# A transformer block on one core: the MLP's first tiles are normed and turned in projection 1, and MLP weights are issued by another queue

## The chip, the cores and the metric

The kernel runs on one core of a Trainium2 chip. Its engines are TensorE (PE, matmuls; PEld is its weight load), VectorE (DVE), ScalarE (ACT), GpSimd (POOL) and SyncE (SP, which only issues transfers). ACT and POOL also issue transfers, each on a queue of its own. The metric is device time in microseconds (us), as the median of several runs. A smaller number is better.

## The reference

One block of a diffusion transformer: x has 2 batches of 2048 tokens with 576 features, in fp32. A condition vector gives six rows (shift, scale and gate for attention and for the MLP).

```
mod = silu(c) @ w_ada + b_ada
sh_msa, sc_msa, g_msa, sh_mlp, sc_mlp, g_mlp = split(mod, 6)
xn = ln(x, 1e-6) * (1 + sc_msa) + sh_msa
q, k, v = (xn @ w_qkv + b_qkv)          # 16 heads of 36
q, k = ln(q) * qn_g + qn_b, ln(k) * kn_g + kn_b
o = softmax(q @ k^T * scale) @ v
x = x + g_msa * (o @ w_proj + b_proj)
xn2 = ln(x, 1e-6) * (1 + sc_mlp) + sh_mlp
x = x + g_mlp * (gelu(xn2 @ w1 + b1) @ w2 + b2)   # 576 -> 2304 -> 576
```

## The kernel before

Tokens are taken in tiles of 128 (16 tiles for each batch, `NT`) and in blocks of four tiles (`TPB` = 4, 512 tokens). The stages run one after the other: inputs of batch 0 (norm, modulation, QKV), attention 0, projection 1 (`outputs(0, ...)`), inputs of batch 1, attention 1, projection 2 (`outputs(1, ...)`), the MLP's first product over all 8 blocks of both batches, and its second product.

**Turning a tile.** A matmul wants the features on the partitions. A tile of rows is therefore measured (`bn_stats` twice, `bn_aggr`, a square root on ACT, a reciprocal), normed in one operation, transposed in squares of 32 x 32 by DVE, and stored to DRAM by four transfers that put the squares in place (`squares_turned`, L894 and L899; the DRAM tile is `turned`). `turned_loaded` (L907, L909) then loads it, transposed, into the tile `xnt` and its tail part by three transfers, and `turned_modulated` applies scale and shift with ACT, and POOL adds the shift of the tail part (L393).

**A projection** (`outputs`) takes token tiles in groups of four, one PSUM tile (`s_tile`, two banks) for each of four; so tile t + 4 can start only when tile t's PSUM has been read. That is done by DVE: `evicted` multiplies the PSUM tile with the gate row into `product` (L1260). `summed` adds `product` to the rows of x1 (x plus bias, gated, which attention prepared in DRAM; L1267), stores x1 (POOL, L1268), and `residual` loads the rows of a later tile (POOL, L1255). The matmuls of a group stand in the order: `whole` of the first two tiles, `halved` of all four (the last 64 features), `whole` of the last two. `placed(t)` runs whatever work another stage has asked to have in between.

**The order of the work.** Inside a `manual_schedule` the named engines run in the order of the code. Elsewhere a scheduler puts each engine's instructions in order. DVE's order is written out in `inputs`, in projection 2 and in the MLP, and during attention also that of POOL and ACT; projection 1 has the scheduler's order on all engines. [...]

**Around the change.** In attention, each pair of heads p, block of queries and group of keys is a step, and `hooks` hang other work on a step. During the last pair of attention 1, `rows_opened` loads the first five tiles of batch 0's x1 back from DRAM, further hooks measure one each, and `rows_turned` at the step (7, NBLK - 1, NG - 1) norms and turns them, with the stores on ACT, SP and POOL in turn. In attention 0 the same hooks do this with the first two tiles of batch 1's x. The rows stand in `spare`, twelve slices of a tile that attention doesn't need by then. Projection 2 keeps x1 in nine `scratch` tiles; between its tiles, DVE forms sums of the MLP's weights: `wb` comes in four quarters of 1152 KB (issued at L1447 on SP, with the loads of the five turned tiles between them) for sums at L1464 to L1467, and `last_rows`, the last 64 rows (576 KB, L1455), is cast and summed at L403 and L404.

**The MLP's first product** has 72 jobs (8 blocks times 9 parts of the hidden features). It uses seven products of sums for four block products, so that DVE forms token sums for every block (`token_sums`, L1511 to L1514), and evicts each job with four operations (L1568 to L1575) ahead of a gelu on ACT and a store by SP. `ahead(job)` loads, turns, reads back and modulates the tiles of the next block, at job numbers given by offsets.

Of the kernel before, what the change touches and what calls it, by code (L numbers as in the profile page):

```python
# [16 lines left out]
P = 128  # L17
# [14 lines left out]
def dit_block(  # L32
# [233 lines left out]

    x_first = const.tile([P, C + 64], F32, name="x_first")

    def rows_normed(pool, xt, repeated=True):
        st = pool.tile([P, 2, 6], F32, name="st", bufs=2)  # L270
        for a in range(2):
            nc.vector.bn_stats(st[:, a, :], xt[:, a * HALF : (a + 1) * HALF])
        mv = pool.tile([P, 2], F32, name="mv", bufs=2)
        nc.vector.bn_aggr(mv, st.rearrange("p a s -> p (a s)"))
        std = pool.tile([P, 1], F32, name="std", bufs=2)
        nc.scalar.activation(std, mv[:, 1:2], AF.Sqrt, bias=eps6)
        rstd = pool.tile([P, 1], F32, name="rstd", bufs=2)
        nc.vector.reciprocal(rstd, std)
        nc.vector.tensor_scalar(xt[:, :C], xt[:, :C], mv[:, 0:1], rstd, ALU.subtract, ALU.mult)  # L279
        if repeated:  # L280
            nc.scalar.copy(xt[:, C:], xt[:, 512:576])
        return xt[:, :512], xt[:, 512:]
# [472 lines left out]
    def block_of_small():  # L755
# [487 lines left out]
                nc.gpsimd.tensor_tensor(rows, rows, spare[2], ALU.add)  # L1243
                nc.gpsimd.dma_start(out=x1_dram[b, (t - 1) * P : t * P, :], in_=rows)

        def outputs(b, weights, between, scratch):


            wp, wp4, g1, pool = weights
            x1s = {}  # L1250

            def residual(t):
                if t < NT:
# [9 lines left out]
            def summed():  # L1263
                while products:
                    t, product = products.pop(0)
                    x1 = x1s.pop(t)
                    nc.vector.tensor_tensor(x1, x1, product, ALU.add)  # L1267
                    nc.gpsimd.dma_start(out=x1_dram[b, t * P : (t + 1) * P, :], in_=x1)  # L1268
                    residual(t + 6)

            def placed(t):
                for do in between.get(t, ()):
# [5 lines left out]
            for t0 in range(0, NT, 4):  # L1278
                tiles, sums = [], []
                for t in range(t0, t0 + 4):  # L1280
                    if t < t0 + 2:
                        placed(t)
                    ps = s_tile()
                    tiles.append(ps)
                    sums.append((
                        [ps[:, a, :HALF] for a in range(2)],
                        lambda k, a, t=t: qo[:, k, t * P : (t + 1) * P],
                        lambda k, a: wp[:, k, a * HALF : (a + 1) * HALF] if k < FULL else wp4[:, 0, :],
                    ))
                    if t < t0 + 2:  # L1290
                        whole(*sums[-1], True)
                summed()
                for i, sum_ in enumerate(sums):
                    halved(*sum_, i >= 2)
                evicted((t0, t0 + 1))
                placed(t0 + 2)
                summed()
                whole(*sums[2], False)
                evicted((t0 + 2,))
                placed(t0 + 3)  # L1300
                whole(*sums[3], False)
                evicted((t0 + 3,))
# [9 lines left out]
        for b in range(B):  # L1312
# [44 lines left out]
            }  # L1357
            if b + 1 < B:
                begun = [(spare[9 + t], x[b + 1, t * P : (t + 1) * P, :], spare[7 + t]) for t in range(2)]
            else:  # L1360
                begun = [
                    (spare[3 + j], x1_dram[0, j * P : (j + 1) * P, :], spare[(8 + j) % len(spare)])
                    for j in range(TPB + 1)
                ]

            def rows_opened():
                opening["begun"] = rows_begun(begun)
                for i in range(len(begun)):
                    opening["begun"][0](i)

            def rows_turned():
                opening["turned"] = opening["begun"][2]()

            hooks |= {(7, 1, 1): rows_opened, (7, NBLK - 1, NG - 1): rows_turned}
            hooks |= {
                (7, 2 + i // NG, i % NG): lambda i=i: opening["begun"][1](i) for i in range(len(begun))
            }
            if b == 0:
                hooks |= {
                    (0, 2, 1): ada_opened,  # L1380
# [12 lines left out]
            if b + 1 < B:  # L1393
                weights, close_weights = input_weights()
                first_turned, rows = opening["turned"]
                xnt = input_loaded(first_turned, nc.sync)
                outputs(b, wp, {12: [lambda: input_modulated(b + 1, xnt)]}, spare)
                close_wp()


# [39 lines left out]
        slot = {1: 0, 2: 2, 3: 3, 4: 6, 5: 4, 6: 5, 7: 1}  # L1440

        wr = [mw.tile([P, MH], F32R, name=f"wr{i}") for i in range(3)]
        rows4, close_rows4 = opened("rows4")
        last_rows = rows4.tile([64, 2, MH], F32, name="last_rows")
        first = opening["turned"]
        for i, (k, f) in enumerate(((0, 0), (0, 1), (1, 0), (1, 1))):
            nc.sync.dma_start(  # L1447
                out=wb[:, i],
                in_=w1[k * PAIR : (k + 1) * PAIR, f * MH : (f + 1) * MH].rearrange("(k p) f -> p k f", p=P),
            )  # L1450
            for j in (2 * i, 2 * i + 1):
                if j <= TPB:
                    n, t = divmod(j, TPB)
                    turned_loaded(xnts[n], slice(t * P, (t + 1) * P), first[j], nc.sync)
        nc.sync.dma_start(out=last_rows, in_=w1[512:576, :].rearrange("p (a f) -> p a f", a=2))  # L1455
        left, right = last_rows[:, 0], last_rows[:, 1]
        last_parts = [
            lambda: weight_parts(wr[0], left),
# [24 lines left out]
            between.setdefault(t + 1, []).append(last_parts[i])  # L1483
        in_order = tc.manual_schedule(engines={mybir.EngineType.DVE})
        in_order.__enter__()
        scratch, close_scratch = opened("scratch")
        outputs(B - 1, wp, between, [scratch.tile([P, C], F32, name=f"x1_{i}") for i in range(9)])
        close_scratch()
        close_rows4()
        close_wp()  # L1490
        close_outs()
        close_xs()
# [89 lines left out]
        def ahead(job):  # L1582
# [3 lines left out]

            def at(**offsets):
                for i in range(TPB):
                    read = max(0, 2 * i - 1)
                    for what, offset in offsets.items():  # L1590
                        m, g = divmod(job - read - offset, HF)
                        if g == 0 and m + 1 < NB and (m, i) > (0, 0):
                            yield what, (m + 1, i)

            for what, todo in at(turn=-2, read=0, modulate=2, load=-5):
                m, i = todo
                block, cols = xnts[m % 2], slice(i * P, (i + 1) * P)
                if what == "load":
# [5 lines left out]
                else:  # L1604
                    turned_modulated(block, cols, 2, m // NBLK)

        for m, k, n in ((2, 0, 0), (5, 1, 1), (3, 0, 1), (4, 1, 0)):
            quarter = w2[k * HF * P : (k + 1) * HF * P, n * HALF : (n + 1) * HALF]
            nc.sync.dma_start(out=ws[m], in_=quarter.rearrange("(f p) c -> p f c", p=P))
        later_sums = [  # L1610
            lambda: nc.vector.tensor_tensor(ws[6], ws[2], ws[3], ALU.add),
            lambda: nc.vector.tensor_tensor(ws[3], ws[3], ws[5], ALU.subtract),
# [8 lines left out]
        rows_ahead = {}  # L1621
        for i in (1, 2):
            rows_ahead[1, i] = mlp_loaded(1, i, nc.gpsimd)
        rows_ahead[1, 1] = tile_turned(rows_ahead[1, 1], nc.gpsimd)
        token_sums(0)
        for job in range(0, NB * HF, 2):
            (n0, f0), (n1, f1) = divmod(job, HF), divmod(job + 1, HF)
# [11 lines left out]
            gelu_stored(n1, f1, 1)  # L1639
            if job % 4 == 2 and job > 2 * HF and later_sums:  # L1640
                later_sums.pop(0)()
            if job == 4 * HF:
                hidden_loaded(0)
        stack.close()
# [139 lines left out]
```

## Time and profile before

| what | us |
|---|---|
| median of 3 runs (lowest to highest) | 3205.18 (3202.65 to 3205.25) |
| the profiled execution | 3209.03 |
| its span in the profile | 3207.2 |
| PE busy | 3159.1 |
| inputs 0, attention 0 | 0 to 254, to 1033.6 |
| projection 1, inputs 1 | to 1105.1, to 1330.8 |
| attention 1, projection 2 | to 2104.5, to 2198.1 |
| MLP's first product, second product | to 2711.6, to 3200.5 |

The stages' bounds are read from PE's timeline. A row of the waits view reads "engine, operation's output, line, what it waited for: us in total, times, longest". A timeline row has the start, the duration, engine and line, operation, tiles and shapes, how many (x), and in brackets the idle time before it with what ended it. A `q` behind an engine's name (SPq) is its issuing of transfers.

### The profile page before, as it was taken

To read this page: it belongs to the slowest core of one execution; us is meant where nothing else is said; L and a number is where in the kernel's file an instruction comes from. 1 tells how busy PE (TensorE), PEld (TensorE's weight loads), DVE (VectorE), ACT (ScalarE), POOL (GpSimd) and SP (SyncE) were. 2 spreads that over 40 slices of the span, in tenths; PEclk is the share of its full clock that TensorE was granted. 3 is DMA by queue.
4 is the path that set the end of the run, shared out by engine and by line. 5 is a ranking of instruction groups with operands and counts; after the bars stand their busy time and mean duration, and the time that the engine had idled before them with its cause. 6 is when DMAs were issued, how large, how long until landed. Compare 5 with 4: busy or idle time off the path is not lost. (4 is left out here: it accounts for less than half of the span.)

```text
span 3207.2 us, 47334 instructions
## 1 busy us (share of the span) xinstructions
PE 3159.1 (98%) x17833; PEld 1895.6 (59%) x17833; DVE 1510.2 (47%) x2213; ACT 1505.3 (47%) x2941; POOL 657.2 (20%) x922
## 2 busy tenths in 40 slices
PE   7999999999999999999999999989999999999999
PEld 5884333333334788633333333357888888777777
DVE  5774333333333478533333333436566554455454
ACT  2336666666666034466666666632555542000000
POOL 4551000111110255300001111023334320122111
PEclk9999999999999999999999999999999999999999
DMA  4222212233222522121222222265555433333331
GB/s 149 76 65 68 75 35 69 62 74 83 65 76 51 169 69 70 39 65 31 50 57 64 66 68 65 64 195 183 151 143 131 132 110 129 133 133 111 118 104 38
DMA packets 163641, 291.51 MB, mean 91 GB/s; under 512 B 43715, under 2 KB 95884, under 8 KB 161292
## 3 DMA queue, kind: packets, MB, share of 16 engines
q1 hardware_dynamic: 112116, 176.37, 18.1%
q0 software_dynamic: 44176, 111.15, 13.4%
q8 instruction: 143, 2.34, 0.3%
q10 hardware_dynamic: 7112, 0.89, 0.2%
q14 instruction: 94, 0.77, 0.1%
HBM read 155.42 MB, written 84.63 MB: 75 GB/s over the span
## 5 line engine op out<-in xcount | busy, mean ns | idle before, releaser
L1127 ACT ACTIVATE pt<-b 128x512 f32<-128x512 f32 x2048 | 1057.6, 610 | 487.0 <-PE b L1136 272.8
L1136 PE MATMUL b<-pt,vt 128*64 128x512 f32 x4096 | 935.0, 598 | 0.0
L1136 PEld LDWEIGHTS b<-pt,vt 128*64 128x64 f32 x4096 | 271.8, 136 | 582.1 <-issue 438.8
L1123 PE MATMUL b<-qm,km 32*128 32x512 f32 x4096 | 568.4, 614 | 0.8 <-DVE vt L1040 0.6
L1184 DVE TENSOR_TENSOR ot<-b,ot 128x512 f32<-128x512 f32 x192 | 132.7, 691 | 643.3 <-PE b L1136 642.9
L1123 PE MATMUL b<-qe,ke 16*128 16x512 f32 x2048 | 423.8, 789 | 0.0
L1029 PE MATMUL s<-wq,xnt 128*128 128x288 f32 x1536 | 405.2, 407 | 6.3 <-DMA wq<-in_w_qkv_dram 5.5
L1123 PEld LDWEIGHTS b<-qm,km 32*128 32x128 f32 x4096 | 191.9, 184 | 270.7 <-ACT pt L1127 208.0
L1696 PE MATMUL s<-ws,as 128*128 128x288 f32 x1440 | 351.8, 406 | 0.0
L1029 PEld LDWEIGHTS s<-wq,xnt 128*128 128x128 f32 x1536 | 281.0, 190 | 68.3 <-DVE xt L279 4.1
L1696 PEld LDWEIGHTS s<-ws,as 128*128 128x128 f32 x1440 | 273.6, 190 | 75.6
L1155 DVE RECIPROCAL den<-den 128x512 f32<-128x512 f32 x64 | 213.5, 3336 | 13.9 <-DMA den<-den_dram 13.9
L1541 PE MATMUL m<-xnt,wb 128*128 128x256 f32 x864 | 211.4, 381 | 4.4 <-DVE cs L1575 3.5
L1541 PE MATMUL m<-s,wb 128*128 128x256 f32 x864 | 211.0, 380 | 2.0 <-DVE s L1511 2.0
L1182 DVE COPY ot<-b 128x512 f32<-128x512 f32 x64 | 44.3, 692 | 331.7 <-PE b L1136 331.7
L899 POOL DMA_DIRECT2D turned<-squares x220 | 147.6, 677 | 222.8 <-DVE squares L894 197.0
L1541 PEld LDWEIGHTS m<-s,wb 128*128 128x128 f32 x864 | 164.7, 191 | 24.9 <-DVE s L1511 2.4
L1123 PEld LDWEIGHTS b<-qe,ke 16*128 16x128 f32 x2048 | 108.3, 184 | 114.5 <-issue 112.7
L1541 PEld LDWEIGHTS m<-xnt,wb 128*128 128x128 f32 x864 | 159.4, 191 | 24.8 <-DVE cs L1575 4.3
L1240 POOL DMA_DIRECT2D kr<-in_x_dram x32 | 17.5, 545 | 720.8 <-DVE met L786 720.8
L1579 ACT ACTIVATE cs<-cs,b_sb 128x512 f32<-128x512 f32 x144 | 99.5, 719 | 113.7 <-DVE cs L1574 90.4
L1696 PE MATMUL s<-ws,hidden 128*128 128x288 f32 x576 | 142.3, 406 | 0.0
(198 smaller groups left out, 2995.6 us busy)
## 6 DMA issues: line engine op xcount, KB each, us to landing
gelu<-cs SPq DMA_DIRECT2D x144, 256.0 KB
hidden<-gelu SPq DMA_DIRECT2D x16, 2304.0 KB
den<-den_dram SPq DMA_DIRECT2D x128, 128.0 KB
turned<-squares POOLq DMA_DIRECT2D x220, 72.0 KB, 2.4
xnt<-turned POOLq DMA_DIRECT2D x56, 256.0 KB, 3.7
x_dram<-kr POOLq DMA_DIRECT2D x48, 288.0 KB, 2.8
qm<-qo SPq DMA_DIRECT2D x192, 64.0 KB
kr<-in_x_dram POOLq DMA_DIRECT2D x34, 288.0 KB, 3.8
```

Source lines behind the costliest of these rows:

```text
L899: queue.dma_start(out=by_square[g], in_=squares[g * SQ : (g + 1) * SQ, :].rearrange("p (k j) -> p k j", j=SQ))
L1029: nc.tensor.matmul(out_a, full[:, k, :], wq[:, k, f], start=k == 0, stop=False)
L1123: nc.tensor.matmul(ps, k[r, keys], q[r, :], start=first, stop=not first)
L1127: nc.scalar.activation(pt[:, h, :], banks[2 * c + h], AF.Exp, scale=SCALE)
L1136: nc.tensor.matmul(acc[64 * h : 64 * h + 64, :], vt[:, v0 : v0 + 64], pt[:, h, :], start=pt is pts[0][0], stop=pt is pts[-1][0],)
L1155: nc.vector.reciprocal(den, den)
L1182: nc.vector.tensor_copy(ot, acc)
L1184: nc.vector.tensor_tensor(ot, acc, ot, ALU.add)
L1240: nc.gpsimd.dma_start(out=spare[t % 2], in_=x[b, t * P : (t + 1) * P, :])
L1541: nc.tensor.matmul(out_m[m], wb[:, slot[m], k, f * P : (f + 1) * P], moving[m](k), start=k == 0 and m in (1, 2, 5, 6), stop=k == 1 and m == 1,
L1579: nc.scalar.activation(part, part, AF.Gelu, bias=b1_sb[:, g : g + 1])
L1696: nc.tensor.matmul(ms[m], stationary[m][:, f, :], ws[m][:, f, :], start=(f == 0), stop=(f == HF - 1))
```

## The change

- `rows_measured` is split from `rows_normed`. `outputs` takes a function `turned_of`; in projection 1 it gives, for tiles 0 to 4, a turning: the tile's x1 is measured after its store is issued, and behind the next `evicted` the new function `turned` norms x1 in place and turns it, with the four stores on POOL. The squares use `spare[9]` to `spare[11]`, and projection 1's x1 rows the first nine of `spare`. DVE's order in projection 1 is now the written one.
- Attention 1 no longer loads, measures and turns these five tiles. In attention 0, the turning of batch 1's two tiles is hung on the step behind the last.
- The MLP's weights `wb` and `last_rows` are issued by ACT; the five loads of turned tiles stay on SP, behind one another.
- The x1 rows of projection 2 are opened ahead of `last_rows`, so they lie where the exponentials (`pt`) of attention were, and `last_rows` lies in memory that is free sooner.
- In the MLP, tile i of the next block is read at job 2i (before max(0, 2i - 1)), modulated one job after (before two). The turn of tile (1, 1) ahead of the first token sums falls out (it comes in job 0). The loads of the four quarters of w2 are written between jobs 2 and 14 and no longer ahead of job 0.

```diff
--- before.py
+++ after.py
@@ -266,7 +266,7 @@
 
     x_first = const.tile([P, C + 64], F32, name="x_first")
 
-    def rows_normed(pool, xt, repeated=True):
+    def rows_measured(pool, xt):
         st = pool.tile([P, 2, 6], F32, name="st", bufs=2)
         for a in range(2):
             nc.vector.bn_stats(st[:, a, :], xt[:, a * HALF : (a + 1) * HALF])
@@ -276,7 +276,11 @@
         nc.scalar.activation(std, mv[:, 1:2], AF.Sqrt, bias=eps6)
         rstd = pool.tile([P, 1], F32, name="rstd", bufs=2)
         nc.vector.reciprocal(rstd, std)
-        nc.vector.tensor_scalar(xt[:, :C], xt[:, :C], mv[:, 0:1], rstd, ALU.subtract, ALU.mult)
+        return mv[:, 0:1], rstd
+
+    def rows_normed(pool, xt, repeated=True):
+        mean, rstd = rows_measured(pool, xt)
+        nc.vector.tensor_scalar(xt[:, :C], xt[:, :C], mean, rstd, ALU.subtract, ALU.mult)
         if repeated:
             nc.scalar.copy(xt[:, C:], xt[:, 512:576])
         return xt[:, :512], xt[:, 512:]
@@ -1243,11 +1247,11 @@
                 nc.gpsimd.tensor_tensor(rows, rows, spare[2], ALU.add)
                 nc.gpsimd.dma_start(out=x1_dram[b, (t - 1) * P : t * P, :], in_=rows)
 
-        def outputs(b, weights, between, scratch):
+        def outputs(b, weights, between, scratch, turned_of=lambda t: None):
 
 
             wp, wp4, g1, pool = weights
-            x1s = {}
+            x1s, to_turn = {}, []
 
             def residual(t):
                 if t < NT:
@@ -1267,6 +1271,14 @@
                     nc.vector.tensor_tensor(x1, x1, product, ALU.add)
                     nc.gpsimd.dma_start(out=x1_dram[b, t * P : (t + 1) * P, :], in_=x1)
                     residual(t + 6)
+                    if turn := turned_of(t):
+                        to_turn.append((turn, x1, rows_measured(xs["pool"], x1)))
+
+            def turned():
+                while to_turn:
+                    turn, x1, scales = to_turn.pop(0)
+                    nc.vector.tensor_scalar(x1, x1, *scales, ALU.subtract, ALU.mult)
+                    turn(x1)
 
             def placed(t):
                 for do in between.get(t, ()):
@@ -1293,10 +1305,12 @@
                 for i, sum_ in enumerate(sums):
                     halved(*sum_, i >= 2)
                 evicted((t0, t0 + 1))
+                turned()
                 placed(t0 + 2)
                 summed()
                 whole(*sums[2], False)
                 evicted((t0 + 2,))
+                turned()
                 placed(t0 + 3)
                 whole(*sums[3], False)
                 evicted((t0 + 3,))
@@ -1357,24 +1371,19 @@
             }
             if b + 1 < B:
                 begun = [(spare[9 + t], x[b + 1, t * P : (t + 1) * P, :], spare[7 + t]) for t in range(2)]
-            else:
-                begun = [
-                    (spare[3 + j], x1_dram[0, j * P : (j + 1) * P, :], spare[(8 + j) % len(spare)])
-                    for j in range(TPB + 1)
-                ]
-
-            def rows_opened():
-                opening["begun"] = rows_begun(begun)
-                for i in range(len(begun)):
-                    opening["begun"][0](i)
-
-            def rows_turned():
-                opening["turned"] = opening["begun"][2]()
-
-            hooks |= {(7, 1, 1): rows_opened, (7, NBLK - 1, NG - 1): rows_turned}
-            hooks |= {
-                (7, 2 + i // NG, i % NG): lambda i=i: opening["begun"][1](i) for i in range(len(begun))
-            }
+
+                def rows_opened():
+                    opening["begun"] = rows_begun(begun)
+                    for i in range(len(begun)):
+                        opening["begun"][0](i)
+
+                def rows_turned():
+                    opening["turned"] = opening["begun"][2]()
+
+                hooks |= {(7, 1, 1): rows_opened, (None, None, None): rows_turned}
+                hooks |= {
+                    (7, 2 + i // NG, i % NG): lambda i=i: opening["begun"][1](i) for i in range(len(begun))
+                }
             if b == 0:
                 hooks |= {
                     (0, 2, 1): ada_opened,
@@ -1394,7 +1403,14 @@
                 weights, close_weights = input_weights()
                 first_turned, rows = opening["turned"]
                 xnt = input_loaded(first_turned, nc.sync)
-                outputs(b, wp, {12: [lambda: input_modulated(b + 1, xnt)]}, spare)
+                first = []
+
+                def turned_of(t):
+                    squares = spare[9 + t % 3]
+                    return (lambda x1: first.append(squares_turned(x1, nc.gpsimd, squares))) if t <= TPB else None
+
+                with tc.manual_schedule(engines={mybir.EngineType.DVE}):
+                    outputs(b, wp, {12: [lambda: input_modulated(b + 1, xnt)]}, spare[:9], turned_of)
                 close_wp()
 
 
@@ -1440,19 +1456,19 @@
         slot = {1: 0, 2: 2, 3: 3, 4: 6, 5: 4, 6: 5, 7: 1}
 
         wr = [mw.tile([P, MH], F32R, name=f"wr{i}") for i in range(3)]
+        scratch, close_scratch = opened("scratch")
+        x1_rows = [scratch.tile([P, C], F32, name=f"x1_{i}") for i in range(9)]
         rows4, close_rows4 = opened("rows4")
         last_rows = rows4.tile([64, 2, MH], F32, name="last_rows")
-        first = opening["turned"]
         for i, (k, f) in enumerate(((0, 0), (0, 1), (1, 0), (1, 1))):
-            nc.sync.dma_start(
+            nc.scalar.dma_start(
                 out=wb[:, i],
                 in_=w1[k * PAIR : (k + 1) * PAIR, f * MH : (f + 1) * MH].rearrange("(k p) f -> p k f", p=P),
             )
-            for j in (2 * i, 2 * i + 1):
-                if j <= TPB:
-                    n, t = divmod(j, TPB)
-                    turned_loaded(xnts[n], slice(t * P, (t + 1) * P), first[j], nc.sync)
-        nc.sync.dma_start(out=last_rows, in_=w1[512:576, :].rearrange("p (a f) -> p a f", a=2))
+        nc.scalar.dma_start(out=last_rows, in_=w1[512:576, :].rearrange("p (a f) -> p a f", a=2))
+        for j in range(TPB + 1):
+            n, t = divmod(j, TPB)
+            turned_loaded(xnts[n], slice(t * P, (t + 1) * P), first[j], nc.sync)
         left, right = last_rows[:, 0], last_rows[:, 1]
         last_parts = [
             lambda: weight_parts(wr[0], left),
@@ -1483,10 +1499,9 @@
             between.setdefault(t + 1, []).append(last_parts[i])
         in_order = tc.manual_schedule(engines={mybir.EngineType.DVE})
         in_order.__enter__()
-        scratch, close_scratch = opened("scratch")
-        outputs(B - 1, wp, between, [scratch.tile([P, C], F32, name=f"x1_{i}") for i in range(9)])
+        outputs(B - 1, wp, between, x1_rows)
+        close_rows4()
         close_scratch()
-        close_rows4()
         close_wp()
         close_outs()
         close_xs()
@@ -1586,13 +1601,12 @@
 
             def at(**offsets):
                 for i in range(TPB):
-                    read = max(0, 2 * i - 1)
                     for what, offset in offsets.items():
-                        m, g = divmod(job - read - offset, HF)
+                        m, g = divmod(job - 2 * i - offset, HF)
                         if g == 0 and m + 1 < NB and (m, i) > (0, 0):
                             yield what, (m + 1, i)
 
-            for what, todo in at(turn=-2, read=0, modulate=2, load=-5):
+            for what, todo in at(turn=-2, read=0, modulate=1, load=-5):
                 m, i = todo
                 block, cols = xnts[m % 2], slice(i * P, (i + 1) * P)
                 if what == "load":
@@ -1604,9 +1618,13 @@
                 else:
                     turned_modulated(block, cols, 2, m // NBLK)
 
-        for m, k, n in ((2, 0, 0), (5, 1, 1), (3, 0, 1), (4, 1, 0)):
+        quarters = [(2, 0, 0), (5, 1, 1), (3, 0, 1), (4, 1, 0)]
+
+        def quarter_loaded():
+            m, k, n = quarters.pop(0)
             quarter = w2[k * HF * P : (k + 1) * HF * P, n * HALF : (n + 1) * HALF]
             nc.sync.dma_start(out=ws[m], in_=quarter.rearrange("(f p) c -> p f c", p=P))
+
         later_sums = [
             lambda: nc.vector.tensor_tensor(ws[6], ws[2], ws[3], ALU.add),
             lambda: nc.vector.tensor_tensor(ws[3], ws[3], ws[5], ALU.subtract),
@@ -1621,7 +1639,6 @@
         rows_ahead = {}
         for i in (1, 2):
             rows_ahead[1, i] = mlp_loaded(1, i, nc.gpsimd)
-        rows_ahead[1, 1] = tile_turned(rows_ahead[1, 1], nc.gpsimd)
         token_sums(0)
         for job in range(0, NB * HF, 2):
             (n0, f0), (n1, f1) = divmod(job, HF), divmod(job + 1, HF)
@@ -1639,6 +1656,8 @@
             gelu_stored(n1, f1, 1)
             if job % 4 == 2 and job > 2 * HF and later_sums:
                 later_sums.pop(0)()
+            if job % 4 == 2 and quarters:
+                quarter_loaded()
             if job == 4 * HF:
                 hidden_loaded(0)
         stack.close()
```

## The prediction

> **What bounds the kernel now.** I read the page's busy shares first, then what TensorE (PE) waits for, then the stages by windows, then every engine's timeline around the waits found.
>
> ```profile
> PE 3159.1 (98%) x17833; PEld 1895.6 (59%) x17833; DVE 1510.2 (47%) x2213; ACT 1505.3 (47%) x2941; POOL 657.2 (20%) x922
> ```
>
> PE is busy in 3159.1 of 3207.2 us. The change removes no matmul, so all it can win is PE's idle time and the time PE runs at a lower clock. The waits view says where the idle time is:
>
> ```profile
> PE s L420 <- DVE product L1260: 17.1, 2, 8.9
> ...
> PE m L1541 <- DVE cs L1575: 3.5, 4, 1.5
> PE m L1541 <- DVE s L1511: 2.0, 1, 2.0
> ```
>
> 17.1 us in two waits stand in projection 2, the rest at the start of the MLP and between its blocks. The windows view has, per stretch, the length, busy time of PE, PEld, DVE, ACT, POOL, then the PE clock, DMA share and GB/s. Projection 1 (1033.6 to 1105.1) and projection 2 (2104.5 to 2198.1) run the same 322 matmuls:
>
> ```profile
> 1033.60:1105.10 71.50, 71.50 (x322) 54.26 (x321) 31.72 (x42) 4.84 (x12) 15.19 (x28) 1.00 0.60 189
> 2104.50:2198.10 93.60, 76.50 (x322) 56.28 (x320) 47.99 (x52) 12.06 (x30) 23.35 (x41) 0.89 0.63 198
> 2133.50:2143.70 10.20, 3.23 (x10) 2.00 (x11) 3.88 (x6) 2.52 (x6) 6.20 (x13) 0.50 0.87 303
> ...
> 2205.20:2208.50 3.30, 3.30 (x9) 2.63 (x8) 2.10 (x6) 1.58 (x2) 1.46 (x3) 0.50 1.04 348
> ```
>
> Projection 2 is 93.60 - 71.50 = 22.1 us longer: 17.1 of waits, and 76.50 - 71.50 = 5.0 of PE time, because after each wait the clock is 0.50 for 10.2 us. Who is late, by VectorE's (DVE) timeline (start, duration, what it waited for):
>
> ```profile
> 2110.23 0.65 DVE L1184 TENSOR_TENSOR ot<-b,ot 128x512 f32<-128x512 f32 x1
> ...
> 2124.72 3.35 DVE L1155 RECIPROCAL den<-den 128x512 f32<-128x512 f32 x1 [10.08 <-DMA den<-den_dram]
> ...
> 2137.74 0.76 DVE L1267 TENSOR_TENSOR x<-x,product 128x576 f32<-128x576 f32 x1 [8.93 <-DMA x<-x_dram]
> ...
> 2165.62 0.75 DVE L403 CAST wr<-last_rows 64x1152 fp32r<-64x1152 f32 x1 [9.88 <-DMA last_rows<-in_w_dram]
> ...
> 2167.93 0.76 DVE L1260 TENSOR_TENSOR product<-s,gate 128x576 f32<-128x576 f32 x1
> ```
>
> DVE runs in written order here. The products that free PE's PSUM tiles stood behind an add that waited 8.93 us for x1 rows, and later behind a cast that waited 9.88 us for MLP weights. So transfers bound it. SyncE's (SP) and GpSimd's (POOL) queues say why they were late:
>
> ```profile
> 2106.25 9.34 SPq L899 DMA_DIRECT2D turned<-kr  x8
> ...
> 2135.16 2.41 SPq L1447 DMA_DIRECT2D wb<-in_w_dram  x4
> 2137.66 1.23 SPq L1455 DMA_DIRECT2D last_rows<-in_w_dram  x1
> ```
> ```profile
> 2133.28 0.45 POOL L393 TENSOR_TENSOR parts<-tail,parts 128x128 fp32r<-128x128 f32 x1 [1.89 <-ACT tail L392]
> 2133.76 1.61 POOL L1255 DMA_DIRECT2D x<-x_dram  x3
> ```
>
> SP spends 9.34 us on the stores of the five turned tiles, then loads these back until 2135, and only then issues the weights. POOL issues the x1 loads behind the modulation's adds, which wait for those loads.
>
> **The Trainium skill.** "TensorE: Matmul & The Clock Gate", Part 1, says that the clock falls to half after an idle window of some 3.4 us and recovers after a busy one. The trace agrees in kind (0.50 after each wait) but not in length: 10.2 us after the long waits, 3.3 after the short pair at the MLP's start (0.90 and 1.96). "DMA: Bandwidth & Descriptors", "Issuing engines are not separate DMA queues": SP and ScalarE (ACT) feed the same 16 engines, so moving an issue saves queueing, not bandwidth; the trace has 0.87 of the engines busy at 303 GB/s in the first slow window. "ScalarE: Activation LUTs", "What ACT_TABLE_LOAD costs": 1283 ns; the trace has 1.28 us.
>
> **What is removed, part by part.** (1) The end of attention 1 loses five loads, five measurings, five norms and transposes of DVE (2103.3 to 2110.2, five times 0.58 + 0.78), and twenty stores. DVE's last ot add then runs at about 2105, not 2110.23. SP is free at about 2104 and issues the xnt loads at once, not between 2120 and 2134. ACT then modulates five tiles from about 2107; at the old pace (five adds of POOL some 2.5 to 3 us apart) that ends at about 2121. POOL's x1 loads follow at 2120.5 rather than 2133.76. The first add came 2137.74 - 2133.76 = 4.0 after; so adds from 2124.5 and product 2 at about 2127. PE first waited at 2140.47 - 8.95 = 2131.5: a margin of 4, gap gone.
>
> (2) The weights wb (four of 1152 KB) follow ACT's modulation, at about 2122 instead of 2135.2. The first sum of two of them ran at 2151.17, 16 after; now about 2138. Four DVE operations behind it (2.56, 1.42, the casts 0.75 and 1.49) put product 7 at about 2146. PE needed it at 2168.74 - 8.12 = 2160.6, which is 2149 to 2150 once the first gap and its slow clock (8.95 + 2.5) are gone: margin about 4. last_rows is no longer awaited (see 4). Projection 2 becomes 71.5: -22.1.
>
> (3) The MLP: the turn of tile (1,1) ahead of the first token sums is gone, a turn being about 3.7 us of DVE by its rows. The 1.96 wait goes, and the 2.0 us that the slow clock added (the first job took 11.0 where others take 7.0: 4.0 less 1.96). Turns of later tiles stand two jobs apart, so no eviction stands behind two of them. In the double turn before 2329, DVE also waited 2.89 for a store (same buffer). The three waits on cs were 0.97, 0.86 and 1.50: -3.3. One turn in 14 us of DVE time has slack, since the gaps came only where two stood together. Total gain: 22.1 + 4.0 + 3.3 = 29.4.
>
> **What is added.** (4) last_rows has memory free early, and the schedule puts its load at the start of attention 1 on ACT, ahead of the exponentials' table load. It waits there for DVE's last v eviction:
>
> ```profile
> 1331.49 1.28 ACT L1127 ACT_TABLE_LOAD   x1
> 1332.79 3.53 ACT L1127 ACTIVATE pt<-b 128x512 f32<-128x512 f32 x7
> ```
> ```profile
> 1331.84 0.69 DVE L1040 TENSOR_TENSOR vt<-s,bq 128x576 f32<-128x576 f32 x1
> ```
>
> The eviction ends at 1332.53; issue 0.6 to 1.3 (ACT's issues take about 0.7 in this trace), then 1.28: first exponential at 1334.4 to 1335.1, 1.65 to 2.35 later. PE fills its eight banks and then waits for it, about 1.9. If the clock falls, up to 1.7 more; 2.3 taken, bounds 0 and 4.
>
> (5) Projection 1 gets the five tiles. Measuring and turning adds 5 x (1.6 + 0.2 + 0.2 + 0.6 + 0.8) = 17 us to DVE's 31.7 of 71.5, which fits by share. It also adds twenty stores of 0.68 to POOL (13.6 on 15.2), each ahead of the x1 stores and loads there. And DVE's order is now written, so a wait holds all that follows. The norm is in place, so it waits until the same tile's x1 store has landed:
>
> ```profile
> 1058.01 0.55 POOL L1268 DMA_DIRECT2D x_dram<-kr  x1
> 1063.70 0.54 POOL L1255 DMA_DIRECT2D kr<-x_dram  x1 [5.14 <-DMA x_dram<-kr]
> ```
>
> There a store took 5.1 to land beside weight loads; the page's median is 2.8. For tiles 0 to 3 the stages' own length (4.5 a tile) covers this. Tile 4's store stands behind eight stores of turned tiles (8 x 0.68 = 5.4) and then lands 2.8 to 5.7 later; product 7, behind that norm on DVE, comes 45.6 to 50.5 us into the stage by adding these up. PE needs it at 45.4 (the place of before's second wait, in an undisturbed stage). Stall 0.3 to 5, middle 2.3; with some slow clock 3.0. Bounds 0 and 10. Later stages inherit nothing, since QKV weights have landed by then. If the cover of the stage is gone, each norm costs what its store needs beyond 4.5.
>
> (6) At no cost: fewer spare rows for x1 (nine for six in flight), the moved hook of batch 1's first two tiles (same operations, one step later, behind the last ot add), and the w2 quarters on SP (idle in the MLP, 144 gelu stores excepted; if not, the second product would wait for ws, and has some 400 us).
>
> Sum: -29.4 + 2.3 + 3.0 = -24.1. Span 3207.2 -> 3183.1; this profiled execution took 3209.03, so it would take 3184.9. The median of the runs is 3205.18, 3.85 below the profiled one: 3181.
>
> **Rivals.** R1, projection 1 takes a wait of the kind removed from projection 2: stores land late beside weights, or product 4's turn waits too. It speaks for it that DMA is 0.60 busy there and DVE's order is now fixed; against it, the slack of four PSUM tiles. 5 to 10 in place of 3: 3183 to 3188, with two slow clock stretches 3191.
> R2, one wait of projection 2 stays: 4.6 MB of weights at 190 to 303 GB/s take 15 to 24 us, and the xnt and x1 loads share that; moving the issue doesn't change it. Margins of 4 speak against it. One wait of 8.95 or 8.12 with its 2.5: 3192; half of one: 3187.
> R3, slower: each of the five norms holds DVE for its store's round trip, which POOL's turned stores delay further. To eat 24.1 more than forecast, each must cost 5.4 beyond the 4.5 covered (five times 5.4 is 27), so stores that land 9.9 after issue. The worst seen beside weight loads is 5.7. From there on: 3205 or more.
> R4, the spread does not do what it says, as the turn still waits for the store or meets the eviction: 3.3 stays, 3184.5.
> R5, the added costs are hidden: 3205.2 - 29.4 = 3176.
>
> **Chances.** Forecast within 4 us of 3181: 0.55 (3177 to 3185). R1 0.14, R2 0.16, R4 0.05, R5 0.06, R3 0.04. All but R3 are faster by more than 0.2% (6.4 us, about what a measurement of this kernel can tell from none): 0.94 faster; 0.02 same and 0.04 slower split R3 and its approach. The range of 3174.5 to 3192 leaves out R3, the worst of R2, and some of R5.
>
> **What would show it.** Right: no wait of L420 on product in projection 2, its clock 1.00, its length 71 to 73; no wait on cs in the MLP; a first MLP job of 7; a PE wait of about 2 on exponentials at the start of attention 1; one of 0 to 5 in projection 1 on a product behind the fifth norm. Wrong: waits on DMA of x or wb ahead of product in projection 2 (R2), or several norms in projection 1 that wait for stores (R1, R3).

## The result, and the profile after

The changed kernel takes 3190.4 us (median of 5 runs, 3187.3 to 3191.1) against 3205.25 (5 runs, 3202.7 to 3207.7): a ratio of 0.9952, interval 0.9937 to 0.9966. That is 14.9 us faster where 24.1 were forecast. The direction was right and the range held the time. But what the forecast had in the range's upper part (R1 and R2) is not what made most of the shortfall, as shown below, so that the range held is in part luck.

The stages, from PE's timeline of the profiled executions (each from its first matmul to the next stage's first, so that projection 2 here is 0.9 longer than in the windows view):

| stage, us | before | after | forecast of the difference | measured |
|---|---|---|---|---|
| start and inputs 0 | 253.2 | 251.0 | 0 | -2.2 |
| attention 0 | 780.4 | 780.3 | 0 | -0.1 |
| projection 1 | 71.5 | 76.2 | +3.0 | +4.7 |
| inputs 1 | 225.7 | 225.4 | 0 | -0.4 |
| attention 1 | 773.6 | 774.8 | +2.3 | +1.2 |
| projection 2 | 94.5 | 72.6 | -22.1 | -21.9 |
| MLP, first product | 512.5 | 512.4 | -7.3 | -0.1 |
| MLP, second product | 489.0 | 489.0 | 0 | 0.0 |
| sum (span 3207.2 to 3188.4) | | | -24.1 | -18.8 |

The profiled execution of before was a long one (3209.03, 3.8 above the median), that of after was not (3190.46); this is why the spans differ by more than the medians do. The start alone differs by 2.2, and in the runs below it moves by as much (249.3 to 254.2) with no edit near it.

The page's shares after, and the view of what PE waits for:

```profile
PE 3157.1 (99%) x17833; PEld 1895.6 (59%) x17833; DVE 1511.4 (47%) x2212; ACT 1514.7 (48%) x2953; POOL 661.8 (21%) x933
```
```profile
PE m L1556 <- DVE s L1526: 4.3, 1, 4.3
PE s L424 <- DVE product L1264: 2.7, 1, 2.7
...
PE b L993 <- ACT pt L1131: 1.4, 1, 1.4
...
PE m L1556 <- DVE cs L1590: 0.5, 1, 0.5
```

The 17.1 us of product waits in projection 2 are gone. The 2.7 that stands under the same name is a wait in projection 1, where before had none. The waits on cs (the tile into which DVE evicts a job) fell from 3.5 to 0.5. But the wait on the first token sum (s) has not gone: it grew from 2.0 to 4.3. The windows of the two projections and of the MLP's start (columns as in the prediction: length, PE, PEld, DVE, ACT, POOL, clock, DMA share, GB/s):

```profile
1031.30:1107.50 76.20, 73.49 (x323) 55.22 (x322) 43.11 (x73) 6.53 (x17) 28.60 (x48) 0.98 0.66 197
2107.60:2179.30 71.70, 71.70 (x322) 54.08 (x320) 42.53 (x43) 11.87 (x30) 18.53 (x35) 1.00 0.70 240
2183.00:2193.50 10.50, 6.23 (x16) 4.93 (x16) 5.05 (x10) 3.23 (x4) 0.62 (x1) 0.68 0.69 246
```

Projection 2 has a PE without a gap at full clock. At the MLP's start, PE is idle for 4.27 of 10.5 us, and its clock is at half for 6.8 us behind the wait (2186.7 to 2193.5), which costs half of that, 3.4.

DVE in projection 2 after the change:

```profile
2129.93 0.76 DVE L1271 TENSOR_TENSOR x<-x,product 128x576 f32<-128x576 f32 x1 [10.79 <-DMA x<-x_dram]
...
2137.88 2.55 DVE L1480 TENSOR_TENSOR wb<-wb 128x2304 f32<-128x2304 f32 x1
...
2142.35 0.74 DVE L407 CAST wr<-last_rows 64x1152 fp32r<-64x1152 f32 x1
...
2144.51 0.76 DVE L1264 TENSOR_TENSOR product<-s,gate 128x576 f32<-128x576 f32 x1
```

The x1 rows are still awaited (10.79), but from 2119 on and not from 2129, so product 2 comes before PE needs it. The sum of wb and the cast of last_rows wait for nothing, and product 7 (2144.51) is 37 us into the stage, where before it was 63.

Now the three waits of after. First the MLP's start. Before, the first token sum stood behind a turn on DVE, and PE waited 1.96 for it:

```profile
2202.34 0.78 DVE L894 STREAM_TRANSPOSE squares<-xt 128x576 f32<-128x576 f32 x1
2203.04 0.65 DVE L1511 TENSOR_TENSOR s<-xnt 128x512 f32<-128x512 f32 x1
```
```profile
2203.75 0.48 PE L1541 MATMUL m<-s,wb 128*128 128x256 f32 x1 [1.96 <-DVE s L1511]
```

After, on DVE, POOL and PE:

```profile
2180.03 1.42 DVE L1271 TENSOR_TENSOR x<-x,product 128x576 f32<-128x576 f32 x2
2186.57 0.69 DVE L1526 TENSOR_TENSOR s<-xnt 128x512 f32<-128x512 f32 x1 [5.12 <-DMA x_dram<-x]
2187.76 0.69 DVE L1527 TENSOR_TENSOR s<-s,xnt 128x512 f32<-128x512 f32 x1 [0.50 <-DMA x_dram<-x]
```
```profile
2181.08 1.21 POOL L1272 DMA_DIRECT2D x_dram<-x  x2 [7.51 <-DVE x L1271]
```
```profile
2187.31 2.93 PE L1556 MATMUL m<-s,wb 128*128 128x256 f32 x6 [4.27 <-DVE s L1526]
```

The first token sum doesn't wait for its inputs but for the stores of x1 rows, issued at 2181. The reason lies in the memory, by the addresses that the built program gives. The sums s1, s2 and s4 lie at bytes 134976 to 141120 of each partition in both kernels, behind cs0 and cs1. The x1 rows of projection 2 are nine tiles of 2304 bytes; before they began at 133952, behind last_rows, so s1 lay over the rows of tiles 9 and 10. After they begin at 124736, and s1 lies over the rows of tiles 13 and 14, and s2 over those of 14 and 15, the last of the stage. The sum may write there only when these rows have been stored.

Projection 1, on DVE, POOL and PE:

```profile
1073.64 0.75 DVE L1264 TENSOR_TENSOR product<-s,gate 128x576 f32<-128x576 f32 x1
1077.29 0.58 DVE L1280 TENSOR_SCALAR kr<-kr,mv,rstd 128x576 f32<-128x576 f32 x1 [2.90 <-DMA x_dram<-kr]
1077.90 0.78 DVE L898 STREAM_TRANSPOSE kr<-kr 128x576 f32<-128x576 f32 x1
1078.61 0.72 DVE L1264 TENSOR_TENSOR product<-s,gate 128x576 f32<-128x576 f32 x1
```
```profile
1068.96 5.34 POOL L903 DMA_DIRECT2D turned<-kr  x8 [4.18 <-DVE kr L898]
1074.29 1.14 POOL L1272 DMA_DIRECT2D x_dram<-kr  x2
```
```profile
1079.38 0.76 PE L424 MATMUL s<-wp,qo 64*128 64x288 f32 x4 [2.71 <-DVE product L1264]
```

The fifth norm waits for its x1 store, which stands behind eight turned stores on POOL. PE needed the product behind it 2.71 us before 1079.38, at 1076.67.

And the start of attention 1, on DVE, ACT and PE:

```profile
1333.84 0.69 DVE L1044 TENSOR_TENSOR vt<-s,bq 128x576 f32<-128x576 f32 x1
...
1334.57 0.52 ACTq L1468 DMA_DIRECT2D last_rows<-in_w_dram  x1
...
1335.28 1.28 ACT L1131 ACT_TABLE_LOAD   x1 [1.81 <-DMA qm<-qo]
...
1336.57 4.03 ACT L1131 ACTIVATE pt<-b 128x512 f32<-128x512 f32 x8
```
```profile
1337.31 0.74 PE L993 MATMUL b<-ident,both 128*128 128x128 f32 x5 [1.36 <-ACT pt L1131]
```

The issue of `last_rows` on ACT follows the end of DVE's last v eviction (1334.53), and the table load and the exponentials stand behind it. So the first exponential starts 2.0 us behind this eviction's end, where before it started 0.26 behind it. The view names a transfer of qm as what the table load waited for; that it was the issue is shown by the run with `last_rows` on SP, below.

### The profile page after: what moved, and what is told of

It is laid out like the page before. It is cut to its first block, busy times and chain, and to the rows that moved or that the text cites. A ratio compares the mean times of both kernels' runs of the same rounds, so it can differ in the third digit from the quotient of the medians.

```text
span 3188.4 us, 47349 instructions
## 1 busy us (share of the span) xinstructions
PE 3157.1 (99%) x17833; PEld 1895.6 (59%) x17833; DVE 1511.4 (47%) x2212; ACT 1514.7 (48%) x2953; POOL 661.8 (21%) x933
## 5 line engine op out<-in xcount | busy, mean ns | idle before, releaser
L1244 POOL DMA_DIRECT2D kr<-in_x_dram x32 | 17.5, 546 | 727.5 <-DVE met L790 727.5
```

## The experiments

Each was timed in several rounds beside the kernel before on the same chip. The medians of before were 3205.7, 3207.3 and 3208.4 in the three groups; ratios are to these. A difference of 2 us between two variants is about what their spreads allow to be read. The changed kernel was not timed again in these groups, so a difference from its 3190.4 also holds what lies between the groups (before's own median moves by 3.1); the stage lengths of the profiled executions are the surer reading.

**The token sums' tiles ahead of cs.**

```diff
-        css = [m1.tile([P, 5, PAIR], F32, name=f"cs{i}") for i in range(2)]
         ss = {m: m1.tile([P, 2, PAIR], F32, name=f"s{m}") for m in (1, 2, 4)}
+        css = [m1.tile([P, 5, PAIR], F32, name=f"cs{i}") for i in range(2)]
```

> The changed kernel, with the token sums' tiles (s1, s2, s4) placed ahead of cs0 and cs1 in the MLP's memory, so that s1 lies over x1 rows of tiles 9 to 11 and not of 13 to 15. Theory A (the first token sum waits for the stores of the last x1 rows, because the memory move put them under s1): the wait of m on s (4.27) and the half clock after it (6.8 us at half speed, 3.4) go; first MLP job near 8; 3190.4 - 7.7 = 3183. Rival B (the sum is late for its inputs, the modulated tiles or the products' end, whatever its address): the wait stays at 2 to 4, 3189 to 3191.

3182.5 us (0.9930, 0.9917 to 0.9944), 7.9 below the changed kernel. On DVE, the sum now follows the add at once:

```profile
2179.08 1.42 DVE L1271 TENSOR_TENSOR x<-x,product 128x576 f32<-128x576 f32 x2
2180.41 0.68 DVE L1526 TENSOR_TENSOR s<-xnt 128x512 f32<-128x512 f32 x1
```

PE has no wait on s and no half clock there, and the MLP's first product takes 504.2 and not 512.4. Only addresses were changed, so the address was the cause. In this profile projection 1 is also 2.4 shorter (its wait is 1.98, without half clock) and attention 1 is 1.4 longer (half clock behind its wait of 1.36), where nothing was edited.

**Turned stores on SP.**

```diff
-                    return (lambda x1: first.append(squares_turned(x1, nc.gpsimd, squares))) if t <= TPB else None
+                    return (lambda x1: first.append(squares_turned(x1, nc.sync, squares))) if t <= TPB else None
```

> The changed kernel, with projection 1's twenty stores of turned tiles issued by SP, not by POOL. Theory A (the fifth norm waits for an x1 store that stands behind eight turned stores on POOL): the wait of 2.71 on product in projection 1 and the 1.7 of half clock go; stage 71.5 to 72; 3190.4 - 4.4 = 3186. Rival B (the store itself lands late, 3 us or more after issue, because the engines are 0.68 busy): the wait stays at 1 or more, 3188 to 3190.

3192.7 us (0.9963, 0.9949 to 0.9976): no gain, and projection 1 took 78.0. The wait for the x1 store became shorter (1.30 for the fifth norm), as theory A said, but another took its place. SP's queue and DVE:

```profile
1060.50 0.35 SPq L875 DMA_DIRECT2D bq<-in_b_qkv_dram  x1
1060.89 19.67 SPq L903 DMA_DIRECT2D turned<-kr  x20
```
```profile
1071.46 0.78 DVE L898 STREAM_TRANSPOSE kr<-kr 128x576 f32<-128x576 f32 x1 [5.67 <-DMA turned<-kr]
```

The stores stood behind a load of the bias, which started only at 1060.5, as DVE ended its last cast from the same buffer. Then they took 0.98 each in the mean on SP (single ones 0.46 to 3.24), where POOL took 0.67 to 0.71. The fourth tile's squares share a buffer with the first's, and its transpose waited 5.67 for that store. PE waited 2.57 for a product and had 6.8 us of half clock. So this run doesn't decide the case; the one with the norm out of place does.

**last_rows on SP.**

```diff
-        nc.scalar.dma_start(out=last_rows, in_=w1[512:576, :].rearrange("p (a f) -> p a f", a=2))
+        nc.sync.dma_start(out=last_rows, in_=w1[512:576, :].rearrange("p (a f) -> p a f", a=2))
```

> The changed kernel, with last_rows issued by SP, not by ACT. Theory A (the issue holds up the exponentials at the start of attention 1): first exponential about 2 us sooner after the last v eviction, the wait of 1.36 gone, attention 1 at 773.6 and not 774.8: 3189.2. Rival B: SP, held by the same wait, delays q and k moves and something else of attention 1 waits: no gain or 1 to 2 lost, 3190 to 3192.

3186.7 us (0.9939, 0.9925 to 0.9952). On ACT, the table load no longer stands behind an issue:

```profile
1331.55 1.28 ACT L1131 ACT_TABLE_LOAD   x1
1332.85 3.54 ACT L1131 ACTIVATE pt<-b 128x512 f32<-128x512 f32 x7
```

The wait on exponentials is gone and attention 1 takes 772.95, 1.8 less. That is more than the 1.2 expected. The medians differ by 3.8, and what goes beyond 1.8 is not shown to be this edit's: the five runs spread over 7 us, and in the profiled one the clock was at half for 3.4 us less at the MLP's start, behind a wait of 4.20 in place of 4.27, and not at all in projection 1, behind one of 1.73.

**These three together.**

> The three edits together: sums ahead, turned stores and last_rows on SP. If the three costs are independent: 3190.4 - 7.7 - 4.4 - 1.2 = 3177. If they hide one another or SP becomes late: above 3180.

3184.1 us (0.9931, 0.9918 to 0.9945). That is above 3180: projection 1 took 78.9 with the stores on SP where the changed kernel takes 76.2, and so gave back 2.7 of the 9.8 that the other two brought (attention 1 773.0, the MLP's first product 504.4).

**The MLP's weights on SP, as before the change.**

```diff
-            nc.scalar.dma_start(
+            nc.sync.dma_start(
                 out=wb[:, i],
...
-        nc.scalar.dma_start(out=last_rows, in_=w1[512:576, :].rearrange("p (a f) -> p a f", a=2))
+        nc.sync.dma_start(out=last_rows, in_=w1[512:576, :].rearrange("p (a f) -> p a f", a=2))
```

> The changed kernel, with all of the MLP's weights (wb and last_rows) issued by SP again, between and behind the loads of the turned tiles as before the change. To be held against the kernel with last_rows alone on SP (3186.7). Theory A (turning in projection 1 is what freed the queues; who issues wb is nothing): wb issued some 2 to 3 later, at about 2123 to 2125, no wait of PE in projection 2, stage 72.6, time 3187 within 2. Rival B (ACT's issuing is needed): product 7 late again, a wait of 2 to 6 with slow clock, 3190 to 3198.

3187.5 us (0.9933, 0.9920 to 0.9947), projection 2 72.6 without a wait of PE. The cast of last_rows waits for nothing:

```profile
2142.86 0.74 DVE L407 CAST wr<-last_rows 64x1152 fp32r<-64x1152 f32 x1
```

With last_rows in early, it does not matter who issues wb.

**The old memory order.**

```diff
-        scratch, close_scratch = opened("scratch")
-        x1_rows = [scratch.tile([P, C], F32, name=f"x1_{i}") for i in range(9)]
         rows4, close_rows4 = opened("rows4")
...
-        outputs(B - 1, wp, between, x1_rows)
-        close_rows4()
-        close_scratch()
+        scratch, close_scratch = opened("scratch")
+        outputs(B - 1, wp, between, [scratch.tile([P, C], F32, name=f"x1_{i}") for i in range(9)])
+        close_scratch()
+        close_rows4()
```

> The changed kernel, with the x1 rows of projection 2 placed behind last_rows again, so that last_rows lies on the exponentials' memory, is loaded behind wb after attention 1, and s1 no longer lies under the last x1 rows. Theory A (the memory move costs at attention 1's start and at the MLP's start, and buys an early last_rows): the waits of 1.36 and 4.27 go (about -1.5 and -7.7), but the cast of last_rows waits in projection 2: landing 20 to 26 after issue at 2123 gives 2143 to 2149 where the cast stands at 2142, so a PE wait of 0 to 4 on product. 3181 to 3187. Rival B (the old memory cost both waits of projection 2): one or both of 8 to 9 return, 3195 or more.

3179.6 us (0.9914, 0.9901 to 0.9928), 10.8 below the changed kernel and below the expected range. The waits of 1.36 and 4.27 are both gone: attention 1 is 1.6 shorter and the MLP's first product 7.3. DVE in projection 2:

```profile
2143.65 0.75 DVE L407 CAST wr<-last_rows 64x1152 fp32r<-64x1152 f32 x1 [2.56 <-DMA last_rows<-in_w_dram]
...
2145.82 0.76 DVE L1264 TENSOR_TENSOR product<-s,gate 128x576 f32<-128x576 f32 x1
```

last_rows, issued at 2123.23, came 20.4 later, and the cast waited 2.56; PE waited for nothing (stage 72.6). In this company, the memory move only cost.

**Only the MLP's part, on the kernel before.**

```diff
-                    read = max(0, 2 * i - 1)
...
-                        m, g = divmod(job - read - offset, HF)
+                        m, g = divmod(job - 2 * i - offset, HF)
...
-            for what, todo in at(turn=-2, read=0, modulate=2, load=-5):
+            for what, todo in at(turn=-2, read=0, modulate=1, load=-5):
...
-        rows_ahead[1, 1] = tile_turned(rows_ahead[1, 1], nc.gpsimd)
```

(with the later loads of w2's quarters)

> The kernel before, with only the MLP's part of the change (tiles two jobs apart, modulation one job after the read, no turn of tile (1,1) ahead of the first token sums). Theory A (as forecast: it frees the first sum and ends the double turns; the changed kernel lost the first of these to its memory move): the wait of 1.96 and the three on cs go, first product 512.5 -> 504 to 505, time 3205.7 - 8 = 3197 to 3198.5. Rival B (the spread gives nothing): 3203 or more.

3198.9 us (0.9976, 0.9966 to 0.9986). What PE waits for, in the parts concerned:

```profile
PE s L420 <- DVE product L1260: 15.3, 2, 9.4
...
PE m L1541 <- issue: 0.9, 1, 0.9
```

No wait on s or cs is left, and the first product takes 504.1, 8.4 less. The forecast for this part (7.3) holds where the rows lie as before.

**The norm out of place.**

```diff
-                    nc.vector.tensor_scalar(x1, x1, *scales, ALU.subtract, ALU.mult)
-                    turn(x1)
+                    nc.vector.tensor_scalar(spare[8], x1, *scales, ALU.subtract, ALU.mult)
+                    turn(spare[8])
...
-                    outputs(b, wp, {12: [lambda: input_modulated(b + 1, xnt)]}, spare[:9], turned_of)
+                    outputs(b, wp, {12: [lambda: input_modulated(b + 1, xnt)]}, spare[:8], turned_of)
```

> The changed kernel, with the norm of the five tiles in projection 1 written to a spare row tile (x1 rows take eight tiles and not nine), so that it doesn't wait for the tile's x1 store. Stores stay on POOL. Theory A (the in-place norm's wait for that store holds the products behind it): the wait of 2.7 on product goes, stage 71.5 to 72, 3190.4 - 4.4 = 3186. Rival B (DVE has too much to do there, or the squares' buffers or the loads of later x1 rows are late): a wait of 1 or more stays, 3188 to 3192.

3186.8 us (0.9936, 0.9922 to 0.9949); projection 1 takes 71.5 again, with all its turning. The fifth norm and the product behind it:

```profile
1072.07 0.57 DVE L1280 TENSOR_SCALAR kr<-kr,mv,rstd 128x576 f32<-128x576 f32 x1
...
1073.38 0.72 DVE L1264 TENSOR_TENSOR product<-s,gate 128x576 f32<-128x576 f32 x1
```

So the wait for the store was the whole of this cost. DVE's added work, 11 us (42.7 in place of 31.7), cost nothing.

**Only the early turning, on the kernel before** (the parts of the diff on projections and hooks; weights, memory and MLP as before).

> The kernel before, with only the turning of the five tiles in projection 1 (and its hooks); weights on SP, the old memory and the old order of the MLP. Theory A (turning earlier alone ends both waits of projection 2): projection 2 72.6 or at most 4 more, projection 1 76, the MLP as before 512; 3206 - 21.9 + 4.7 = 3189, up to 3193. Rival B (two of turning, issuing by ACT and the memory move together are needed): a wait on the cast of last_rows or on wb of 4 or more comes back, 3194 to 3200.

3193.4 us (0.9952, 0.9939 to 0.9966), just past theory A's range. Projection 2 takes 81.2: the first wait is gone and the second is not. DVE:

```profile
2155.13 0.75 DVE L407 CAST wr<-last_rows 64x1152 fp32r<-64x1152 f32 x1 [12.98 <-DMA last_rows<-in_w_dram]
2155.91 1.35 DVE L408 TENSOR_TENSOR wr<-last_rows,wr 64x1152 fp32r<-64x1152 f32 x1
2157.30 0.76 DVE L1264 TENSOR_TENSOR product<-s,gate 128x576 f32<-128x576 f32 x1
```

```profile
PE s L424 <- DVE product L1264: 7.8, 2, 5.4
```

PE waited 5.41 for that product, with half clock behind it (the other wait in this row is projection 1's). So rival B was partly right: the early turning ends the first wait alone, while for the second one more thing is needed, either last_rows early (the weights on SP with the memory moved) or the weights on ACT (the old memory). Each alone is enough, beside the early turning, and the change has both. No run has these two without the early turning, so that the turning can't be left out is not shown. Why last_rows took 29.7 from issue to landing here and 20.4 from ACT's queue was not separated: counted from the stage's start, its issue was even 0.6 sooner here, wb's 3.4 later, and from 2125 to 2145 the DMA engines were busy all the time in both (shares of 1.00 to 1.03).

**Both ways to a better kernel.** The memory move kept and its costs mended (token sums ahead, last_rows on SP, norm out of place), and the memory move left out (old order, weights on ACT, norm out of place):

> The changed kernel with its memory move kept and all three costs mended: token sums' tiles ahead, last_rows on SP, norm out of place. Theory A (the three costs are independent): projection 1 71.5, attention 1 773, MLP's first product 504 to 505; 3190.4 - 7.9 - 1.8 - 4.7 = 3176. Rival: one comes back as another wait, above 3179.

> The changed kernel with the x1 rows of projection 2 behind last_rows again and the norm out of place. Theory A: projection 1 71.5, projection 2 72.6, attention 1 773, MLP 504 to 505, so 3179.6 - 4.7 = 3175, the same as with the memory move kept and mended (an early last_rows is worth nothing). Rival B: the cast of last_rows is closer to its limit (it waited 2.6), a wait on product in projection 2 of 1 or more: 3177 or more.

3176.3 (0.9901, 0.9886 to 0.9916) and 3177.8 (0.9904, 0.9889 to 0.9919). Their stages agree within 0.2 in all but the start and inputs 0: projection 1 71.5, attention 1 772.9 and 773.0, projection 2 72.6, the MLP's first product 504.1 in both. The costs were independent: by the stages of the profiled executions 4.7 + 1.8 + 8.3 = 14.8 less in the first, and its median is 14.1 below the changed kernel's. The two can't be told apart. Either beats the kernel before by 1.0% and the changed kernel by about 0.4%. In the first, PE has this left in the 3140 us behind its last wait for the QKV weights:

```profile
PE m L1556 <- issue: 0.9, 1, 0.9
...
PE b L1127 <- DVE vt L1044: 0.6, 1, 0.6
```

## Why the prediction was right or wrong

**Parts 1 and 2, projection 2 (-22.1, measured -21.9): right**, by its own chain. Relative to the stage's start, x1 loads were issued 15 us in (forecast 16, before 29), wb 13 to 15 (forecast 17.5, before 31), product 7 done at 38 (forecast 42). PE had no wait and full clock. The claim that last_rows would be landed long before held too. The prediction did not weigh that turning, issuing and memory do one thing between them; the runs showed that the turning ends the first wait alone, and that for the second one of the other two is spare. It also has the clock at half for 10.2 us after each wait. By the clock's record these stretches began at 2133.5 and 2164.2, within the waits, so that only 3.2 and 5.7 us of PE's work fell into them; its 5.0 for both was taken from PE's busy time and holds.

**Part 4, attention 1 (+2.3, measured +1.2): mechanism right, size over.** The exponential was 1.8 later (forecast 1.65 to 2.35); PE waited 1.36 and the clock did not fall in this execution. The 1.2 is a net: in the seven other runs that turn early and do not have ACT issue last_rows there, attention 1 takes 772.9 to 773.1, so this issue cost 1.8, and 0.5 was gained that the forecast did not have.

**Part 5, projection 1 (+3.0, measured +4.7): mechanism right, down to the tile.** Product 7 was done 48.1 us into the stage (forecast 45.6 to 50.5) where PE needed it at 45.4. The mis-sized terms were the wait, 2.71 where 2.3 was taken, and above all the half clock, 1.7 where 0.7 was; 0.3 is not located. DVE's added work was over-counted at 17 us without harm: the two `bn_stats` of a tile take 0.8 together and not 1.6.

**Part 3, the MLP (-7.3, measured -0.1): wrong.** The step that failed is "The 1.96 wait goes, and the 2.0 us that the slow clock added". The turn ahead of the sums did go, and where only that is done it brings what was forecast. But the change also moved the x1 rows. That part was costed for what it did to last_rows, and what lies on the rows' new place next was not asked. It was the token sums, so a wait of 4.27 with 3.4 lost to half clock stood where 1.96 had been with 1.7 (2.0 in the prediction). The other half of this part, the three waits on cs, was right: 3.3 became 0.5, and before that 0.5 DVE had not two turns but a wait of 8.66 for a gelu store, in the 14 us after SP had issued a load of 2304 KB of hidden rows (2263.1); what held that store was not tried.

So of the 9.2 us by which the gain fell short, 7.2 are the MLP's part: the step named rose by 4.0 where it was to fall by 4.0, and the rest of the part gave 0.8 more than its 3.3. Projection 1 is 1.7 and projection 2 0.2, less 1.1 that was put down too much for attention 1. The rest, 1.2, is within the spread of the runs. R3, the slower side, did not come about: the store's round trip held up one norm enough to reach PE, not five.

## What to carry to other kernels

When a tile is moved in memory, look at both neighbours in time: what lay there before sets when the tile can be filled, and what is placed there next waits until its last use, a store included, has ended. An in-place operation behind a store waits for that store and for what stands ahead of it on its queue (here eight stores, 5.34 us); a spare tile cost nothing here and gave 4.7 us in its stage. And before a change that has several cures for one wait is kept whole, each should be tried without the others: one of them here only cost.

## What was not expected of the hardware

The half clock behind a wait of PE is not a function of the wait alone. The trace of after shows none behind 1.36, but the run with the sums ahead shows 3.4 us of it behind 1.36 at the same place. Waits of 1.73, 1.98 and 2.47 in projection 1 had none, one of 2.35 had 3.4 and one of 2.57 had 6.8. At the MLP's start waits of 4.20, 4.22 and 4.36 had 3.4, and 4.27 and 4.53 had 6.8. A wait of 1.96 there had 3.4 in before and none in the run with only the early turning.

The traces show what it also hangs on. Leaving out the end of each, all stretches of half clock in the thirteen traces last one to four times 3.413 us, and all changes of the clock in one trace lie whole multiples of this step apart. So each trace can be cut into such steps. Behind its start, in the projections and the MLP, a step at full clock in which PE was busy for 1.50 us or less was always followed by half clock, and one in which it was busy for 1.58 or more never was. (At the start of attention 1 the clock fell once, after 1.89.) The wait of 2.47 lay over two steps (PE busy 2.63 and 1.72) and cost nothing more; that of 2.35 lay mostly in one (PE busy 1.34). In the step of the two waits of 1.96, PE was busy for 1.45 and for 1.58. Where the steps lie differs from execution to execution. So a wait of two to four us costs its length and from nothing to 3.4 more, and part of this is chance.

The time of a store's issue is not one number for each queue. In the run with the turned stores on SP, the twenty took 0.46 to 3.24 us each there, and the busier POOL took 0.67 to 0.71 in after. Why SP's are so uneven is open.
